# A four-layer gated transformer on one core: the conditional expert blocks of layer 0 moved ahead of the sure ones, three blocks added by one-hot matrices, and parts moved off GpSimd

## Chip, core and metric

The kernel runs on one core of a Trainium2 chip (trn2). The metric is the device time of one launch in microseconds (us). The engines are TensorE (PE; its weight loads are PEld), VectorE (DVE), ScalarE (ACT), GpSimd (POOL) and SyncE (SP, which here only issues transfers).

## The reference

The input x has 1024 rows of 256 numbers; four layers each add a gated attention to 64 context rows and a gated feed-forward (FFN) network. All is float32.

```python
for n in range(4):
    x = x + tanh(g_xattn[n]) * xattn[n](layernorm(x), ctx)
    x = x + tanh(g_ffn[n]) * ffn[n](layernorm(x))
```

- Layers 0 and 1: attention over a latent of 64 numbers, 16 heads. Layers 2 and 3: ordinary attention, 16 heads of 16, causal.
- FFN 0: a mixture of 16 experts of width 176. A softmax over the scores, a bias, the best 6 experts of each row, and two shared halves for all rows: `y = sum_e c[:, e] * ((silu(x W1 + B1) * (x W3 + B3)) W2 + B2)`.
- FFN 1: `gelu(x w1_q + b1) w2_q + b2`, the weights made ternary: `sign(w)` where `|w| >= 0.7 * mean|w|`, else 0; hidden width 1024.
- FFN 2: 8-bit weights and 8-bit rows: `round(x / s) @ round(w / t) * s * t + bias`, with `s = max|x| / 127` for each row.
- FFN 3: 8 experts of width 512, the best 2 of each row, and a shared expert.

## The kernel before

The stream x stays in SBUF as 8 tiles of 128 rows (`stream`, `x[t]`), two groups of four. The kernel is written in a tile framework that works out semaphores and buffer slots. It also orders the instructions of each engine at compile time, by priority in the order of the program, so an instruction may stand ahead of its place in the text where its inputs and slot are free. What is fixed is that each engine, and each queue of transfers, then runs in that order and waits at its first unready instruction. `behind(later, sooner)` orders two instructions by hand. The inside of a `tc.If` is ordered as one piece; all engines load the value and either run the piece or jump over it.

**The experts of layer 0.** Each row goes to 6 of 16 experts. The (row, expert) pairs are sorted on the chip into blocks of 128 rows of one expert: at least 55 blocks are never less than needed for this shape of data (`SURE0 = 55`), and up to 63 could be. `Experts.run(sure)` unrolls the sure blocks and then, under `tc.If(used > sure)`, the eight others; with these inputs the branch is jumped over. For each block:

- `fetch`: an indirect DMA on POOL gathers 128 rows with their 16 weights (`xs`), four blocks ahead.
- `turn`: PE transposes the rows, DVE copies them (`st`), DVE picks the block's weight, and PE loads the expert's address into a register (`value_load`).
- `up`: the bias as a one-hot product, two matmuls, SiLU on ACT, the product on DVE.
- `turn_hidden` and `down`: transpose, copy, the output product; the output `y` is copied into a ring of two times four tiles, and an indirect DMA on POOL adds it to rows in DRAM (`sums`). Layer 0 has two such sums, for even and odd blocks. The sum of the even ones starts as x plus the shared expert (`keep_rows`); blocks that add to the same sum wait for each other's landing.

Beside the blocks run steps of `fold1` (products of layer 1's attention weights, which PE makes) and of `ternary1` (layer 1's FFN weights made ternary on DVE: eight reductions of 128x512, one tiny matmul, then eight compares and eight selects). `between(i)` takes the next step after block i. After the branch both sums are read back into SBUF, on the queues of SP and ACT, added on DVE, and layer 1 begins.

Weights arrive through three slots of 1 MB (`C`): `used(name)` frees one and issues the next load on SP. PSUM tiles are `ps_mm` (one bank, four of them) and `ps_wide` (two banks, two of them).

**Attention.** `in_flight(scores, attend, gate, beside)` runs over the 8 tiles with three in flight: scores on PE, maximum and difference on DVE, exponential on ACT, sum and reciprocal on DVE, the product with it on POOL (L438), transposes on PE, copies on ACT, output products on PE. `beside` is work taken one step a tile.

**FFN 1.** The hidden layer is held as three bfloat16 terms whose sum is the float32 value (`three_terms`, L1491): the first term is a cast on ACT (L1493), the rest a subtraction on POOL (L1494), the second term a cast on DVE (L1495), the third a subtraction on DVE (L1496). The input of group 1 (`inputs(1)`) is prepared in the third quarter of group 0's up phase (L1557).

**FFN 2.** For each group: normalise on ACT, add the bias to the stream on POOL (L1634), the largest value of each row and its reciprocal on DVE (L1638 to L1640), scale and round on DVE (L1643, L1644), transposes, products (L1649), and the product with the row's scale is added to the stream (L457).

Of the kernel before, what the change touches and what calls it, by code (L numbers as in the profile page):

```python
# [37 lines left out]
P = 128  # L39
# [29 lines left out]
SURE0, SURE3 = 55, 20  # L69
W0U = 4 * F0  # L70
# [12 lines left out]
def tile_flamingo(ctx: ExitStack, tc: tile.TileContext, a: dict, out: bass.AP):  # L83
# [39 lines left out]
    def small(shape, name, bufs=3):  # L123
        return sb.tile(shape, F32, tag=name, name=name, bufs=bufs)
# [709 lines left out]
    def attention1(gate):  # L834
        weff, wvo = kept.pop("fold1")
        qcT = latents()
# [14 lines left out]
        latent_attend(qcT, wvo, gate, beside=queries(1))  # L851
# [133 lines left out]

    def keyed(layer, gate):
        beside = iter(())
        if layer == 2:
            values = region("wqk", 2048, "values")
            for _ in keys_values(2, region("weff", 2048, "kbd2"), values[:, :1024]):  # L990
                pass
            beside = keys_values(3, region("wvo", 2048, "kbd3"), values[:, 1024:])
# [175 lines left out]
    class Experts:  # L1168


        def __init__(self, route, xd, n, nb, stride, width, chunk, sums, w, bias, hTs, between):
# [4 lines left out]
            self.between = between  # L1176
            self.ring = [sb.tile([P, 4, D], F32, tag="xT", name="ring", bufs=2) for _ in range(2)]
# [5 lines left out]
        def fetch(self, b):  # L1183

            xs = sb.tile([P, D + self.experts], F32, tag="xn", name="xs", bufs=6)
# [8 lines left out]
        def turn(self, b):  # L1194
            st = t4([P, 1024], "blk")
            ps = ps_mm()
            for c in range(2):
                nc.tensor.transpose(ps[:, c * P : (c + 1) * P], self.xs[b][:, c * P : (c + 1) * P], ident)  # L1198
            nc.vector.tensor_copy(st[:, :D], ps[:, :D])  # L1199
# [15 lines left out]
                self.offset[0:1, b : b + 1], min_val=0, max_val=self.stride * (self.w.shape[1] // self.stride - 1)  # L1215
            )

        def up(self, b):
# [28 lines left out]
            nc.vector.scalar_tensor_tensor(s, lin, self.weight.pop(b), s, ALU.mult, ALU.mult)  # L1247
# [10 lines left out]
        def down(self, b):  # L1258
# [11 lines left out]
            if b % 2:  # L1270
                nc.vector.tensor_copy(y, ps[:, :D])
            else:
                nc.scalar.copy(y, ps[:, :D])  # L1273
            nc.gpsimd.indirect_dma_start(  # L1274
# [7 lines left out]
        def run(self, sure):  # L1282

            self.blocks(0, sure, self.between)
            used = nc.values_load(self.used, min_val=0, max_val=self.nb)
            with tc.If(used > sure):
                self.blocks(sure, self.nb, lambda i: None)

        def blocks(self, first, last, between):
            for b in range(first, min(first + 4, last)):  # L1290
                self.fetch(b)
            for i in range(first, last + 2):
                if i + 4 < last:
                    self.fetch(i + 4)
# [26 lines left out]
    def ffn0(gate):  # L1321
# [63 lines left out]
        used("L0_s13")  # L1385
        used("L0_s2")
# [11 lines left out]
        ternary = ternary1()  # L1398

        def between(i):  # L1400
            if i % 3 == 2 and not ended:
# [4 lines left out]
            if i > 32 and ended:  # L1406
                next(ternary, None)

        moe = Experts(placing, xd, E0, NB0, W0, F0, FC0, sums0, big[:, : E0 * W0], (bias_0, choice), hTs, between)
        moe.run(SURE0)  # L1410
        kept["fold1"] = ended[0]
        for t in range(NT):
            if t % TPG == 0:
                tiles = slice(t, t + TPG)
                nc.sync.dma_start(out=stream[:, tiles, :], in_=tiled(sums0[0], 0)[:, tiles, :])
                more = t4([P, TPG, D], "more")
                nc.scalar.dma_start(out=more, in_=tiled(sums0[1], 0)[:, tiles, :])
            if t % 2 == 0:
                two, its = slice(t, t + 2), slice(t % TPG, t % TPG + 2)
                done = nc.vector.tensor_tensor(stream[:, two, :], stream[:, two, :], more[:, its, :], ALU.add)  # L1420
        load_experts3(0, EARLY3, done)
        for _ in ternary:
            pass

    def ffn3(gate):
# [57 lines left out]
        moe = Experts(route[0], xd, E3, NB3, W3, F3, P, sums3, big, None, hTs, lambda i: None)  # L1483
        moe.run(SURE3)

# [5 lines left out]
    def three_terms(terms, v, rest):  # L1491

        nc.scalar.copy(terms[0], v)  # L1493
        nc.gpsimd.tensor_tensor(rest, v, terms[0], ALU.subtract)  # L1494
# [317 lines left out]
```

## Time and profile before

| | |
|---|---|
| device time, median of 3 runs | 948.43 us (945.85 to 948.74) |
| the profiled execution | 947.2 us, its span 945.4 us |
| mean granted clock of PE | 0.959 |
| busy: PE, PEld, DVE, ACT, POOL | 844.9, 547.3, 514.0, 288.7, 344.5 us |
| DMA | 75.15 MB, 38762 packets |

The stages, in us from the start of the span, as the rows of the timeline give them: attention 0 to about 212, routing and shared expert to 268, the sure blocks of layer 0 to 448, the sums read back to 475, attention 1 to about 570, FFN 1 to 625, attention 2 to 690, FFN 2 to 709, attention 3 to 760, FFN 3 to the end.

How to read the profile. "Busy" is the time in which an instruction of the engine ran; a matmul's end is modelled, so a busy PE is not a PE at its peak. A row of the timeline has start and duration in us, the engine, the line of the kernel, the operation, the tiles it writes and reads, the shapes, the number of instructions merged into the row, and in brackets the idle time of the engine before it and what ended it. A float32 matmul is two instructions in these rows, so that `x16` is eight products; a transpose is one. SPq, ACTq and POOLq are the queues in which transfers are issued.

### The profile page before, as it was taken

To read this page: it belongs to the slowest core of one execution; us is meant where nothing else is said; L and a number is where in the kernel's file an instruction comes from. 1 tells how busy PE (TensorE), PEld (TensorE's weight loads), DVE (VectorE), ACT (ScalarE), POOL (GpSimd) and SP (SyncE) were. 2 spreads that over 40 slices of the span, in tenths; PEclk is the share of its full clock that TensorE was granted. 3 is DMA by queue.
4 is the path that set the end of the run, shared out by engine and by line. 5 is a ranking of instruction groups with operands and counts; after the bars stand their busy time and mean duration, and the time that the engine had idled before them with its cause. 6 is when DMAs were issued, how large, how long until landed. Compare 5 with 4: busy or idle time off the path is not lost. (4 is left out here: it accounts for less than half of the span.)

```text
span 945.4 us, 12712 instructions
## 1 busy us (share of the span) xinstructions
PE 844.9 (89%) x4464; PEld 547.3 (58%) x4467; DVE 514.0 (54%) x1299; ACT 288.7 (31%) x561; POOL 344.5 (36%) x262
## 2 busy tenths in 40 slices
PE   5999999999999998899089997899869899999994
PEld 4544335876667875676045873665545556666662
DVE  4666457756934344573146765778777865222220
ACT  2221004433222332233013436516545531122221
POOL 0455452310066777787201232502312402144321
PEclk9999999999999998999589999989989999999997
DMA  9200228101156555654570000180000011122223
GB/s 359 93 16 22 79 65 258 52 18 32 56 158 161 125 121 128 156 86 71 117 266 1 1 1 1 42 302 2 1 23 1 1 47 58 40 47 48 38 23 66
DMA packets 38762, 75.15 MB, mean 79 GB/s; under 512 B 6240, under 2 KB 26706, under 8 KB 37322
## 3 DMA queue, kind: packets, MB, share of 16 engines
q1 hardware_dynamic: 23562, 52.01, 16.4%
q0 software_dynamic: 14496, 20.47, 12.9%
q10 hardware_dynamic: 640, 1.84, 0.5%
q8 instruction: 39, 0.64, 0.3%
q14 instruction: 25, 0.20, 0.1%
HBM read 58.73 MB, written 16.61 MB: 80 GB/s over the span
## 5 line engine op out<-in xcount | busy, mean ns | idle before, releaser
L438 POOL TENSOR_TENSOR attn<-attn,sm 128x1024 f32<-128x1024 f32 x32 | 60.8, 1901 | 197.1 <-DVE sm L437 163.9
L1247 DVE SCALAR_TENSOR_TENSOR blk<-wide,weight,blk 128x176 f32<-128x176 f32 (+1 forms) x75 | 37.0, 494 | 138.0 <-ACT blk L1246 137.9
L1274 POOL DMA_INDIRECT sums<-ring,big x55 | 87.5, 1590 | 34.9 <-issue 10.8
L422 PE MATMUL wide<-xT,big 128*128 128x512 f32 x192 | 88.3, 610 | 0.3 <-ACT big L557 0.3
L684 DVE TENSOR_TENSOR rope<-wide,big 128x512 f32<-128x512 f32 x96 | 59.6, 684 | 48.8 <-PE wide L422 47.5
L1227 PE MATMUL wide<-big,blk 128*128 x220 | 77.0, 472 | 0.1
L1186 POOL DMA_INDIRECT xs<-xd,big x55 | 55.1, 1001 | 55.8 <-DMA sums<-x 35.6
L1238 PE MATMUL wide<-big,blk 128*128 x160 | 72.2, 593 | 0.5 <-DVE blk L1199 0.5
L1246 ACT ACTIVATE blk<-wide 128x176 f32<-128x176 f32 (+1 forms) x75 | 29.4, 392 | 122.5 <-PE wide L1238 60.2
L422 PEld LDWEIGHTS wide<-xT,big 128*128 128x128 f32 x192 | 35.8, 193 | 47.6 <-issue 41.3
L657 PE MATMUL mm<-vo,attnT 128*128 128x256 f32 x256 | 58.6, 382 | 0.9 <-ACT attnT L453 0.9
L1262 PE MATMUL mm<-big,blk 88*128 x220 | 57.6, 384 | 0.5 <-ACT blk L1255 0.5
L407 PE MATMUL mm<-ident,xn 128*128 128x128 f32 x112 | 19.9, 322 | 41.5 <-DVE xn L395 35.4
L657 PEld LDWEIGHTS mm<-vo,attnT 128*128 128x128 f32 x256 | 47.4, 190 | 8.7 <-ACT attnT L453 2.9
L453 ACT COPY attnT<-mm 128x512 f32<-128x512 f32 x64 | 34.6, 589 | 54.7 <-PE mm L452 54.2
L1262 PEld LDWEIGHTS mm<-big,blk 88*128 88x128 f32 x220 | 42.0, 192 | 16.0 <-ACT blk L1255 1.4
L1227 PEld LDWEIGHTS wide<-big,blk 128*128 128x128 f32 x220 | 40.7, 196 | 13.3 <-issue 1.2
L436 DVE TENSOR_REDUCE sm<-attn 128x16 f32<-128x1024 f32 x32 | 38.8, 1213 | 16.3 <-ACT attn L430 13.7
L1186 POOL DMA_INDIRECT xs<-xd,scratch x20 | 19.5, 973 | 76.2 <-PE mm L1198 54.0
L1274 POOL DMA_INDIRECT sums<-ring,scratch x20 | 31.5, 1573 | 39.2 <-ACT ring L1273 16.8
L1238 PEld LDWEIGHTS wide<-big,blk 128*128 128x128 f32 x160 | 28.8, 190 | 28.9 <-issue 28.2
L407 PEld LDWEIGHTS mm<-ident,xn 128*128 128x128 f32 x112 | 15.1, 162 | 47.2 <-ACT rstd L383 27.6
(321 smaller groups left out, 1704.3 us busy)
## 6 DMA issues: line engine op xcount, KB each, us to landing
big<-in_L_w_gate_up SPq DMA_DIRECT2D x8, 1024.0 KB, 8.2
big<-in_L_w SPq DMA_DIRECT2D x4, 1408.0 KB, 7.9
big<-in_L_w_down SPq DMA_DIRECT2D x8, 512.0 KB, 9.3
w_L_qk<-in_L_qk SPq DMA_DIRECT2D x4, 896.0 KB, 8.7
big<-in_L_w SPq DMA_DIRECT2D x4, 704.0 KB
big<-in_L_wo SPq DMA_DIRECT2D x1, 2048.0 KB, 12.9
xd<-xn SPq DMA_DIRECT2D x16, 128.0 KB, 1.8
sums<-x SPq DMA_DIRECT2D x16, 128.0 KB, 1.8
```

The lines of the kernel that those rows point to most:

```text
L407: nc.tensor.transpose(ps[:, i * P : (i + 1) * P], n[:, c * P : (c + 1) * P], ident)
L422: nc.tensor.matmul(ps, w(c), xT[:, c, :], start=(c == 0), stop=(c == 1))
L436: nc.vector.tensor_reduce(sm, e, AX.X, ALU.add)
L438: nc.gpsimd.tensor_tensor(e, e, sm.unsqueeze(2).to_broadcast([P, groups, n]), ALU.mult)
L657: nc.tensor.matmul(ps[:, :D], aT[:, s, :], vo[:, s, :], start=(s == 0), stop=(s == NP - 1))
L684: nc.vector.tensor_tensor(m[:, s, :].rearrange("q (b t) -> q b t", t=S), ps[:, s, :].rearrange("q (b t) -> q b t", t=S), table, ALU.mult,)
L1186: nc.gpsimd.indirect_dma_start(out=xs, out_offset=None, in_=self.xd, in_offset=bass.IndirectOffsetOnAxis(ap=self.gather[:, b : b + 1].bitc ...
L1227: nc.tensor.matmul(ps[:, 0, : 2 * n], st[:, c * P : (c + 1) * P], self.w[:, bass.ds(r + c * 2 * n, 2 * n)], start=False, stop=(c == 1),)
L1238: nc.tensor.matmul(ps[:, k, :n], st[:, c * P : (c + 1) * P], self.w[:, bass.ds(r + (2 * c + k) * n, n)], start=(c == 0), stop=(c == 1),)
L1247: nc.vector.scalar_tensor_tensor(s, lin, self.weight.pop(b), s, ALU.mult, ALU.mult)
L1262: nc.tensor.matmul(ps[:, :D], hT[:, j * P : (j + 1) * P], self.w[: self.chunk, bass.ds(r + j * D, D)], start=(j == 0), stop=(j == self.n - 1),
L1274: nc.gpsimd.indirect_dma_start(out=self.sums[b % len(self.sums)], out_offset=bass.IndirectOffsetOnAxis(ap=self.scatter[:, b : b + 1].bitca ...
```

## The change

- `run` fetches the first four blocks, loads `used`, puts the `tc.If` with the eight rare blocks there, and runs the sure blocks after it (layer 0 alone, `hot > 0`; layer 3 keeps its order). Rare blocks are fetched one at a time into a slot of their own.
- In both expert layers the offsets of eight blocks at a time are copied into a small tile (`near`) behind the copy of the block's rows, and the register is loaded from it.
- The outputs of the last three sure blocks of layer 0 (`HOT0`) are not scattered. `hit` makes a one-hot matrix of 128 x 8 x 128 for each, beside blocks 27, 32 and 37; `collect` reads both sums back, all on SP, and adds them; `add` multiplies the one-hot matrices with the three outputs, two tiles of the stream to a PSUM bank, and adds the product to the stream.
- `ternary1` moves from the sure blocks to attention 1. `fold1` takes a step every fourth block from block 5, not every third. `used` of the shared expert's two weights comes after block 3.
- `three_terms` subtracts on DVE and casts every second second term on ACT; `inputs(1)` comes one quarter sooner.
- FFN 2: the rounding of group 0 is taken into the steps beside attention 2; the row's scale is multiplied in before the transposes, the bias is a one-row matmul in front of the products, and nothing is on POOL.

```diff
+HOT0 = 3
     def attention1(gate):
+        ternary = ternary1()
-        latent_attend(qcT, wvo, gate, beside=queries(1))
+        latent_attend(qcT, wvo, gate, beside=zip_longest(queries(1), ternary))
+        for _ in ternary:
+            pass
...
+    def beside2(keys):
+        for i in range(NT + 3):
+            if i == NT + 1:
+                kept["rounded"] = rounded(0)
+            next(keys, None)
+            yield
...
     class Experts:
         def turn(self, b):
-            nc.vector.tensor_copy(st[:, :D], ps[:, :D])
+            copied = nc.vector.tensor_copy(st[:, :D], ps[:, :D])
+            if b < self.sure and b % 8 == 0:
+                n = min(8, self.sure - b)
+                self.near = small([1, 8], "near", 2, I32)
+                behind(nc.vector.tensor_copy(self.near[:, :n], self.offset[0:1, b : b + n]), copied)
+            offset = self.near[:, b % 8 : b % 8 + 1] if b < self.sure else self.offset[0:1, b : b + 1]
...
         def down(self, b):
+            if b in self.hits:
+                self.held.append((self.hits.pop(b), y))
+                return
...
+        def hit(self, b, room, after=None):
+            base, step = self.rows
+            row, at = small([P, 1], "row"), small([P, NT], "at")
+            copied = nc.vector.tensor_copy(row, self.scatter[:, b : b + 1])
+            nc.vector.tensor_scalar(at, base, row, -1.0 / step, ALU.subtract, ALU.mult)
+            for h, first in room:
+                n = h.shape[1]
+                nc.vector.tensor_tensor(
+                    h,
+                    place.unsqueeze(1).to_broadcast([P, n, P]),
+                    at[:, first : first + n].unsqueeze(2).to_broadcast([P, n, P]),
+                    ALU.is_equal,
+                )
+            return room
...
+        def add(self, held):
+            for t in range(0, NT, 2):
+                ps = ps_mm()
+                for u in (t, t + 1):
+                    for i, (hits, y) in enumerate(held):
+                        h = next(h[:, u - v, :] for h, v in hits if v <= u < v + h.shape[1])
+                        at = (u - t) * D
+                        nc.tensor.matmul(ps[:, at : at + D], h, y, start=(i == 0), stop=(i == len(held) - 1))
+                two = stream[:, t : t + 2, :]
+                nc.vector.tensor_tensor(two, ps.rearrange("p (u d) -> p u d", u=2), two, ALU.add)
...
-        def run(self, sure):
-            self.blocks(0, sure, self.between)
+        def run(self, sure, collect=None):
+            self.sure = sure
+            for b in range(4):
+                self.fetch(b)
+            if not self.hot:
+                self.blocks(0, sure, self.between, 4)
             used = nc.values_load(self.used, min_val=0, max_val=self.nb)
             with tc.If(used > sure):
-                self.blocks(sure, self.nb, lambda i: None)
+                self.blocks(sure, self.nb, lambda i: None, 0)
+            if self.hot:
+                self.blocks(0, sure, self.between, 4)
+                collect()
+                self.add(self.held)
...
     def ffn0(gate):
-        used("L0_s13")
-        used("L0_s2")
         def between(i):
-            if i % 3 == 2 and not ended:
+            if i == 3:
+                used("L0_s13")
+                used("L0_s2")
+            if i > 4 and i % 4 == 1 and not ended:
 ...
-            if i > 32 and ended:
-                next(ternary, None)
+        def collect():
+            more = [t4([P, TPG, D], "more") for _ in range(NG)]
+            for g in range(NG):
+                nc.sync.dma_start(out=stream[:, groups[g], :], in_=tiled(sums0[0], 0)[:, groups[g], :])
+            for g in range(NG):
+                nc.sync.dma_start(out=more[g], in_=tiled(sums0[1], 0)[:, groups[g], :])
+            for t in range(0, NT, 2):
+                two, its = slice(t, t + 2), slice(t % TPG, t % TPG + 2)
                added.append(
                    nc.vector.tensor_tensor(stream[:, two, :], stream[:, two, :], more[t // TPG][:, its, :], ALU.add)
                )
...
     def three_terms(terms, v, rest, scalar):
         nc.scalar.copy(terms[0], v)
-        nc.gpsimd.tensor_tensor(rest, v, terms[0], ALU.subtract)
-        nc.vector.tensor_copy(terms[1], rest)
+        nc.vector.tensor_tensor(rest, v, terms[0], ALU.subtract)
+        (nc.scalar.copy if scalar else nc.vector.tensor_copy)(terms[1], rest)
         nc.vector.tensor_tensor(terms[2], rest, terms[1], ALU.subtract)
...
-                if g == 0 and f2 == 2:
+                if g == 0 and f2 == 1:
                     xT.append(inputs(1))
-                three_terms([hidden[:, g, k, 2 * f2 : 2 * f2 + 2, :] for k in range(3)], h, h)
+                three_terms([hidden[:, g, k, 2 * f2 : 2 * f2 + 2, :] for k in range(3)], h, h, f2 % 2 == 1)
...
+    def rounded(g):
...
+            nc.vector.tensor_scalar(n, n, xi[:, i : i + 1], ROUND, ALU.mult, ALU.add)
+            nc.vector.tensor_scalar(n, n, ROUND, xs[:, i : i + 1], ALU.subtract, ALU.mult)
...
     def ffn2(gate):
-            nc.gpsimd.tensor_tensor(tiles, tiles, bias_2.unsqueeze(1).to_broadcast([P, TPG, D]), ALU.add)
-                nc.vector.tensor_scalar(n, n, xi[:, i : i + 1], 127.0, ALU.mult, ALU.min)
-                nc.vector.tensor_scalar(n, n, ROUND, ROUND, ALU.add, ALU.subtract)
+            xqT = transposed(kept.pop("rounded") if g == 0 else rounded(g))
+                nc.tensor.matmul(ps[:, :D], ones[:1], bias_2, start=True, stop=False)
-                gated_add(g * TPG + i, ps[:, :D], xs[:, i : i + 1])
+                nc.vector.tensor_tensor(x[t], ps[:, :D], x[t], ALU.add)
```

## The prediction

> **What bounds the kernel now.** I read the 40 slices of the page first: TensorE (PE) is busy in tenths of 9 almost throughout, except in the slice from 449 us, where its digit is 0, in two 8s from 354 us, and in a 7, two 8s and a 6 between 567 and 709 us. So what the change is worth has to come from these places or from the layer-0 expert loop in front of slice 19. Next I read busy time by stretch, the columns being PE, PEld, DVE, ACT, POOL, clock, DMA share, GB/s:
>
> ```profile
> 268.00:300.00 32.00, 31.18 (x208) 23.11 (x209) 11.89 (x46) 8.26 (x23) 18.26 (x17) 0.95 0.69 188
> 340.00:400.00 60.00, 53.47 (x256) 37.62 (x256) 26.22 (x89) 16.16 (x45) 43.84 (x35) 0.94 0.61 135
> 448.40:475.50 27.10, 0.00 (x0) 0.02 (x1) 6.44 (x23) 2.19 (x4) 6.24 (x5) 0.54 0.52 125
> 570.20:602.70 32.50, 24.33 (x101) 10.54 (x104) 18.44 (x22) 21.29 (x32) 11.50 (x6) 0.95 0.00 1
> ```
>
> The 55 sure blocks run from 268 to 448.3 us. PE is full until 340 (40.00 of 40 from 300 on); after that it loses 6.5 us in 60. POOL carries two indirect DMAs a block (gather about 1.0 us, scatter 1.59, each after 0.30 of issue: 3.2 us a block), PE 2.65 us a block plus the fold of layer 1. The two are close, and POOL falls behind. From 448.3 to 475.5 PE does nothing. The timeline says why:
>
> ```profile
> 448.33 0.37 ACT L1273 COPY ring<-mm 128x256 f32<-128x256 f32 x1 [1.22 <-PE mm L1262]
> 448.94 1.55 POOL L1274 DMA_INDIRECT sums<-ring,big  x1 [0.50 <-issue]
> ...
> 456.54 1.55 POOL L1274 DMA_INDIRECT sums<-ring,big  x1 [1.17 <-DMA sums<-ring,big]
> 462.12 0.81 SPq L1415 DMA_DIRECT2D x<-sums  x2
> ...
> 468.47 1.29 DVE L1420 TENSOR_TENSOR x<-x,more 128x512 f32<-128x512 f32 x2 [21.75 <-DMA more<-sums]
> ...
> 475.51 2.10 PE L407 MATMUL mm<-ident,xn 128*128 128x128 f32 x8 [27.21 <-DVE xn L395]
> ```
>
> The last output leaves PSUM at 448.7, but four scatters are still queued on POOL; the last one starts at 456.54, the sums are read back at 462.12, landed at 468.47, normalised, and PE starts again. That chain ends last here.
>
> **Part by part,** against the profiled execution (span 945.4, device time 947.2; the median shown is 948.43, 1.2 more).
>
> **Three blocks not scattered, no branch behind them.** Blocks 52 to 54 stay in SBUF, so POOL's last scatter is block 51, which today starts at 448.94 (four remain after the copy: 51, 52, 53, 54). Chain: 448.94 + 3.9 (median landing of L1274) = 452.8; read-back 6.35 (462.12 to 468.47) gives 459.2; then the 7.04 us from there to PE, and two to four more adds of 128x512 (L1420, 0.69 each) = 467.6 to 469.0 against 475.5. That is 6.5 to 7.9 us won. The four loads now stand all on SP, where the two of the even sums go as soon as block 50 has landed; I count 0. The one-hot product is 8 tiles x 3 blocks x 2 passes of 0.216 us (L657: 16 in 3.46 us) = 10.4 us of PE, from 448.7 to 459.1: hidden by the wait for the read-back that ends at 459.2. If that cover is gone, the 10.4 us are themselves the tail, and it lasts to about 461 instead of 475.5 (15 less). The three hits are 1.2 us each on DVE (a 128x1024 operation, L429), which idles half of the loop. Taken -7, bounds -3 (landing as slow as the 5.6 us from 456.54 to 462.12, adds all in front) and -15.
>
> **The branch ahead.** All engines load `used` (ready at 231.4, L1144) and jump over eight unrolled blocks between the fourth gather and block 0. Nothing in the trace shows a jump alone. In layer 3 SP and ACT issue 2.26 us after POOL's last scatter has ended (936.76 to 939.02), in layer 0 4.03 us after (458.09 to 462.12), with a landing in both: the jump costs 0 to 4. On the other side, if engines join there with everything the skipped blocks need (the stored rows L372 of 267.49 land 6.1 us later, at 273.6) and jump then, block 0 starts at 277.6 instead of 268.8: +9. PE waits for it, and behind POOL's jump queue the gathers 4 and up. Taken +3, by the row of layer 0 (4.0) less the idle of 1.0 us that PE has at 267.94 today.
>
> The Trainium skill (Runtime: NRT & Kernel Launch, Instruction fetch mechanics) says that a taken branch to a target outside the two pages held forces a fetch before execution goes on; that speaks against moving a jump from a place covered by a DMA wait to one that is not. It gives no time for the stall, so by it the term is above 0 and no more.
>
> **Layer-1 ternary weights out of the loop.** 8 reductions (0.68), 8 compares (0.52), 8 selects (0.75), small ones 0.8: 16.4 us of DVE leave the loop. What they cost there is POOL, in two ways:
>
> ```profile
> 389.90 1.61 POOL L1274 DMA_INDIRECT sums<-ring,big  x1 [3.10 <-DVE sums L1513]
> ...
> 415.50 1.79 POOL L1274 DMA_INDIRECT sums<-ring,big  x1 [0.30 <-DVE blk L1247]
> ```
>
> The reduction waits 3.3 us for its weights and holds everything behind it in DVE's queue, so a scatter starts 2.8 late; and five gathers and scatters between 414 and 425 take 0.1 to 0.2 more than their fellows at 0.99 and 1.59 (0.8 in sum). Loop -4; bounds 0 (PE is the pace then) and -8 (with the 3.6 us that the clock of 0.94 costs in 340 to 400). Fold steps every fourth block instead of third move PE work, not its amount. In attention 1 the 16.4 us meet 14.0 us of idle DVE up to 500 and 17.1 up to 557, while PE is full: +1, bounds 0 and +5 (a third of it in front of a softmax).
>
> **Late registers.** One copy of 8 integers on DVE per 8 blocks, at 0.2 us; PE then loads a register after that copy, not long before. Taken 0 (seven of eight values are there early); see the rivals.
>
> **Loads moved on SP.** `used` of the two shared-expert weights now comes after block 3, so two loads of the fold's inputs (issued at 255.25 and 265.76, 7.6 us to landing) go out between 270, when their slots are free, and 280, and land by 288; the first fold step comes with block 5, near 287. Taken 0; a late landing holds PE by up to 3, within the bounds of the branch. With the fold ending at block 49, the loads for layers 1 and 2 go out up to 40 us later and stand in SP's queue ahead of the read-back, behind the slot that the last fold step frees, about 14 us before the last block. Taken 0: the read-back waits for block 50's scatter anyway.
>
> **FFN 1 without GpSimd.** Two groups by line of DVE, and then two rows of PE's timeline:
>
> ```profile
> L1496 DVE TENSOR_TENSOR big<-h,big 128x1024 bf16<-128x1024 f32 x8 | 13.4, 1672 | 0.2
> L1495 DVE CAST big<-h 128x1024 bf16<-128x1024 f32 x8 | 11.2, 1404 | 12.2 <-POOL h L1494 12.2
> ```
>
> ```profile
> 586.27 1.02 PE L1565 MATMUL mm<-xT,w_L_w 128*128 128x512 bf16 x4 [3.45 <-DVE more L1548]
> ...
> 596.27 0.81 PE L1565 MATMUL mm<-more,w_L_w 128*128 128x512 bf16 x3 [1.68 <-DVE more L1550]
> ```
>
> The same cast takes 0.69 alone and 2.6 beside L1494 on POOL; the subtraction 1.22 and 3.03. That is 9.3 us of DVE in which it stands still: (11.2 - 8 x 0.69) + (13.4 - 8 x 1.22). Now DVE takes the eight subtractions itself (+9.8) and gives four casts to ACT (-2.8 on DVE, +4.2 on ACT). DVE's total falls by only 2.3, but L1548 and L1550 no longer stand behind a stalled cast: the two PE waits go, 5.1 us, and with them part of the 3 us in which matmuls run 0.43 instead of 0.215 apart after 586. Against it stands ACT, 2.35 to 3.4 us per pair of feature blocks beside PE's 2.58. Taken -5, bounds -1 (ACT is next) and -9.
>
> **FFN 2.** Group 0 is rounded within attention 2, the bias becomes a one-row matmul, and POOL's 2.34 us adds (L1634) go.
>
> ```profile
> 691.03 1.48 DVE L1639 TENSOR_SCALAR xs<-xs 128x4 f32<-128x4 f32 x1
> ...
> 693.72 1.96 PE L407 MATMUL mm<-ident,xn 128*128 128x128 f32 x8 [4.44 <-DVE xn L1644]
> ```
>
> L1639 takes 1.48 here, beside L1634 on POOL, and 0.16 in group 1: 1.3 us on the path. The wait of 4.44 in front of group 0's transposes is what its earlier rounding can take away; group 1's chain then no longer queues behind it on DVE (1.7 us, L384 at 694.62 after the root at 692.93). Added: 8 x 2 x 0.216 = 3.5 us of bias matmuls, half under the wait for group 1, and 4.2 us of DVE within attention 2, where DVE is busy 46 of 62 us. Taken -4, bounds 0 and -7.
>
> Sum: -7 + 3 - 4 + 1 + 0 - 5 - 4 = -16; 947.2 - 16 = 931.2, and with the profiled run 1.2 under the median, 932. The bounds, taken as independent, give 920 to 942.
>
> **Rivals.** *The front eats the tail:* the branch costs its +9 and the loop stays POOL's; -7 + 9 + 0 + 1 - 5 - 4 = -6, 942. For it: PE has no other work at 268; against: the register is known 36 us before. *PE sets the pace:* POOL keeps up, block 51 has landed before the last block is done, and only the 10.4 us of one-hot matmuls remain: -15 + 3 - 6 + 1 - 5 - 4 = -26, 922. Against it: 7 scatters remain after the last gather at 434.03, at 2.1 us each. *Slower, by the late registers:* if each `value_load` now stands on PE between the transposes and the matmul that uses it and waits for DVE, every block of both expert layers pays a hand-over. The smallest hand-overs to PE in the loop are 0.20 to 0.53 us (L1253 after L1247); at 0.33 x 75 blocks this is 25 us: 932 + 25 = 957. It decides from 16 / 75 = 0.21 us a block. Against it: eight offsets come with one copy, and PE's loop shows no gap for register loads today.
>
> **Numbers.** Forecast 0.46, front 0.20, PE's pace 0.12, late registers 0.22. Measured differences under 0.3% (2.8 us) count as none. Faster: 0.45 of the forecast, 0.15 of the front case, all of PE's pace, 0.72. Same: 0.01, 0.03, and 0.03 of the late registers, 0.07. Slower: the rest, 0.02 of the front case and 0.19 of the late registers. The range must take in the forecast and the front case, the upper half of PE's pace and the lower part of the late registers: 919 to 954.
>
> **What would show it.** Right: the last L1274 of layer 0 within 1 us of PE's last block, one-hot matmuls behind it, PE's gap of 27.2 down to about 20, less the 10.4 that they fill; the cast L1495 at 0.69 each; no POOL row in FFN 2. Wrong: PE idle for over 4 us between the shared expert and block 0, more than 2.8 us a block where there is no fold, PE waits for DVE in attention 1 that are not there now, or ACT as releaser of L1565.

## The result, and the profile after

The changed kernel takes 942.69 us in the median of 20 runs (935.47 to 949.27), the kernel before 948.59 (945.25 to 959.39): ratio 0.9937, 95% interval 0.9921 to 0.9954, some 6 us faster. The forecast was 932, 16 faster: the sign and the range held, the size did not. Three later comparisons, each on a chip of its own, gave 0.9963 (0.9935 to 0.9991), 0.9941 (0.9913 to 0.9968) and 0.9929 (0.9900 to 0.9959).

First the stages that the prediction was built on, as busy time by stretch of the changed kernel; columns as before (PE, PEld, DVE, ACT, POOL, clock, DMA share, GB/s).

```profile
267.20:300.00 32.80, 29.41 (x147) 20.82 (x149) 11.71 (x49) 7.67 (x22) 19.65 (x17) 0.86 0.55 120
340.00:400.00 60.00, 57.21 (x299) 42.70 (x298) 28.27 (x100) 17.41 (x49) 45.79 (x35) 1.00 0.61 132
452.70:465.90 13.20, 10.35 (x49) 8.79 (x47) 7.14 (x19) 1.95 (x3) 0.00 (x0) 1.00 0.67 229
566.20:592.40 26.20, 23.67 (x102) 11.09 (x104) 20.90 (x28) 23.23 (x33) 0.00 (x0) 0.93 0.00 1
```

The gap behind the last block is 13.2 us instead of 27.1, and 10.35 of it is work; the up phase of FFN 1 is 26.2 us instead of 32.5 with no POOL in it. So two stages gained more than the whole change did. Where did it go? One profile each is too little for that, so the next table has the stages of two profiles of the kernel before and of four of the changed kernel, cut at TensorE's rows (first transposes of a layer, first product of a phase).

| stage, us | before | changed | mean difference | forecast |
|---|---|---|---|---|
| start to layer 1's first transpose | 475.5, 476.5 | 465.9, 468.1, 467.7, 465.8 | -9.1 | -8 |
| attention 1 | 94.7, 95.0 | 100.3, 100.5, 100.1, 100.5 | +5.5 | +1 |
| FFN 1 | 54.5, 54.6 | 47.3, 46.2, 46.2, 46.2 | -8.0 | -5 |
| attention 2 | 64.6, 64.6 | 64.7, 64.0, 65.9, 64.0 | 0 | 0 |
| FFN 2 | 20.8, 20.9 | 22.4, 26.6, 22.4, 26.6 | +3.7 | -4 |
| attention 3 | 51.4, 51.4 | 51.4, 51.5, 54.5, 51.5 | +0.8 | 0 |
| FFN 3 to the end | 184.0, 184.0 | 185.2, 186.7, 186.3, 188.1 | +2.6 | 0 |
| span | 945.4, 946.8 | 937.2, 943.8, 943.0, 942.7 | -4.4 | -16 |

Attention 1 and FFN 2 hold 12 of the missing 12 us; layer 3 adds 3, FFN 1 and layer 0 gave 4 more than forecast. Now the lines behind each. The end of layer 0, in the timeline of the changed kernel:

```profile
448.79 1.54 POOL L1300 DMA_INDIRECT sums<-ring,big  x1 [0.79 <-PE mm L1276]
...
450.42 1.10 SPq L1479 DMA_DIRECT2D x<-sums  x2
...
452.50 10.53 PE L1334 MATMUL mm<-ring,hits 128*128 128x256 f32 x48
...
453.03 0.81 SPq L1481 DMA_DIRECT2D more<-sums  x2
...
458.69 2.50 DVE L1485 TENSOR_TENSOR x<-x,more 128x512 f32<-128x512 f32 x4 [7.60 <-DMA more<-sums]
...
465.88 1.64 PE L409 MATMUL mm<-ident,xn 128*128 128x128 f32 x8 [2.85 <-DVE xn L397]
```

The last scatter leaves at 448.79, while the last block still runs; its landing and the read-back end at 458.69 and are covered by the one-hot products. This is the chain that the prediction wrote down, within 2 us of it at every step (its 448.94, 452.8, 459.2 and 467.6 stand beside the rows at 448.79, 453.03, 458.69 and 465.88).

Attention 1, its last 20 us, same view:

```profile
547.16 0.28 PE L1596 MATMUL mm<-sums,ones 128*128 128x2 f32 x2
...
549.50 3.18 DVE L1600 TENSOR_SCALAR nthr<-thr 128x2 f32<-128x2 f32 x1
...
552.72 0.49 DVE L1605 TENSOR_SCALAR low<-w_L_w,nthr 128x512 f32<-128x512 f32 x1
...
563.40 0.48 DVE L1605 TENSOR_SCALAR low<-w_L_w,nthr 128x512 f32<-128x512 f32 x1
563.54 1.12 PE L1701 MATMUL mm<-ident,wq 128*128 128x128 f32 x4 [5.20 <-DVE wq L1695]
```

The eight reductions were done by 478.5, but the tiny product that makes the threshold of them stands in TensorE's order at 547.16, in step with the tiles. So all eight comparisons and selections come behind it, from 552.72 to 564.86, mixed with the weights of layer 2, and TensorE waits 5.20 us for VectorE, a wait that is not there before.

FFN 2, TensorE's rows:

```profile
682.08 0.69 PE L1732 MATMUL mm<-kept,ones 1*128 1x256 f32 x2
682.70 1.13 PE L1734 MATMUL mm<-kept,xT 128*128 128x256 f32 x4
...
688.29 0.44 PE L409 MATMUL mm<-ident,xn 128*128 128x128 f32 x2 [2.77 <-DVE xn L1721]
688.65 0.69 PE L1732 MATMUL mm<-kept,ones 1*128 1x256 f32 x2
689.28 0.69 PE L409 MATMUL mm<-ident,xn 128*128 128x128 f32 x2
689.90 1.22 PE L1732 MATMUL mm<-kept,ones 1*128 1x256 f32 x2
```

The first half no longer waits (4.44 us before), the second does: 2.77 us. One of the one-row products of the bias falls into the rest of that wait (688.65); the others cost 0.52 to 0.63 us each (682.08 to 682.70), and one 1.15 at the half clock that follows.

### The profile page after: what moved, and what is told of

It reads as the page before. It is cut to its first block, busy times and chain, and to the rows that moved or that the text cites. A ratio compares the mean times of both kernels' runs of the same rounds, so it can differ in the third digit from the quotient of the medians.

```text
span 937.2 us, 12881 instructions
## 1 busy us (share of the span) xinstructions
PE 858.9 (92%) x4528; PEld 558.2 (60%) x4531; DVE 521.8 (56%) x1328; ACT 292.3 (31%) x565; POOL 315.7 (34%) x247
## 4 chain that ended last, share of the span: by engine, by line
PE 72%; DVE 12%; DMA 5%; ACT 4%; issue 3%; POOL 2%; SPq 0%; POOLq 0%; ACTq 0%; DVEq 0%
PE wide L424 9%; PE wide L1261 7%; PE mm L1285 7%; PE wide L1250 6%; PE mm L424 4%; PE mm L659 4%; PE wide L1529 2%; PE mm L1662 2%; PE wide L644 2%; PE mm L1646 2%; DMA sums<-ring,big 2%; PE mm L454 2%; PE mm L1276 2%; PE wide L940 2%; PE mm L1216 2%
## 5 line engine op out<-in xcount | busy, mean ns | idle before, releaser
L1300 POOL DMA_INDIRECT sums<-ring,big x52 | 83.2, 1599 | 28.8 <-issue 10.0
L1250 PE MATMUL wide<-big,blk 128*128 x220 | 79.4, 479 | 11.0 <-DVE near L1221 6.5
L1261 PE MATMUL wide<-big,blk 128*128 x160 | 72.6, 594 | 2.5 <-DMA sums<-x 2.1
L1204 POOL DMA_INDIRECT xs<-xd,big x55 | 54.6, 992 | 60.3 <-DMA sums<-x 35.7
L1250 PEld LDWEIGHTS wide<-big,blk 128*128 128x128 f32 x220 | 40.9, 198 | 26.2 <-issue 15.4
L1217 DVE COPY blk<-mm 128x256 f32<-128x256 f32 x75 | 31.4, 420 | 16.7 <-PE mm L1216 13.3
L454 PE MATMUL mm<-ident,attn 128*128 128x128 f32 x256 | 34.7, 280 | 6.2 <-POOL attn L440 6.1
```

What stands on the lines that cost most here:

```text
L454: nc.tensor.transpose(ps[:, i * P : (i + 1) * P], ev[:, pr * P : (pr + 1) * P], ident)
L1204: nc.gpsimd.indirect_dma_start(out=xs, out_offset=None, in_=self.xd, in_offset=bass.IndirectOffsetOnAxis(ap=self.gather[:, b : b + 1].bitc ...
L1250: nc.tensor.matmul(ps[:, 0, : 2 * n], st[:, c * P : (c + 1) * P], self.w[:, bass.ds(r + c * 2 * n, 2 * n)], start=False, stop=(c == 1),)
L1261: nc.tensor.matmul(ps[:, k, :n], st[:, c * P : (c + 1) * P], self.w[:, bass.ds(r + (2 * c + k) * n, n)], start=(c == 0), stop=(c == 1),)
L1300: nc.gpsimd.indirect_dma_start(out=self.sums[b % len(self.sums)], out_offset=bass.IndirectOffsetOnAxis(ap=self.scatter[:, b : b + 1].bitca ...
```

## The experiments

Each kernel differs from the changed one by its edit alone, unless it says otherwise. The ratio is to the kernel before, on the same chip.

**The changed kernel again** (three chips), and the kernel before for a second profile. The "wait at block 48" is a wait of TensorE, in front of an up product, for the register that comes out of the copied offsets (`near`); its rows follow under "Registers straight from the list".

> The changed kernel again, beside its variants. Ratio to before 0.992 to 0.995. Theory (the order of each engine is fixed, so its waits come back): TensorE waits 4 to 6 us for the small copy of offsets at block 48, and attention 1 lasts 99 to 101 us. Rival (the wait at block 48 was one execution's chance, a landing that was late once): that wait is under 2 us here, and the loop is 3 us or more shorter than its 185.4.

> The changed kernel beside the next kernels. All theories: ratio 0.993 to 0.997, layer 1 starts at 465 to 471 us, attention 1 lasts 99 to 101, the up phase of FFN 1 25 to 27.

> The changed kernel beside it. All theories: ratio 0.993 to 0.997; attention 1 99 to 101 us, layer 1 starts at 465 to 471.

> The kernel before, for a second profile of its stages. All theories: attention 1 94 to 96 us, FFN 1 up 32 to 33, FFN 2 20.5 to 21.5, layer 1 starts 19 us after the last scatter, at 473 to 479.

Medians 945.81, 942.97 and 944.08 us; the ratios and the stages are above. The wait at block 48 came back each time (5.6 to 6.0 us): it is in the order of the engines, not chance. What differs from run to run is FFN 2 (22.4 or 26.6) and attention 3 (51.4 or 54.5); the last section says by what.

**The threshold first.**

```diff
+        any(next(ternary) for _ in range(9))
         latent_attend(qcT, wvo, gate, beside=zip_longest(queries(1), ternary))
```

> The reductions, the tiny product and the first comparison of the ternary weights are taken ahead of attention 1's tiles. Theory (the tiny product stood at the end of TensorE's order, so all comparisons came when the stage was ending): the product moves from 547 us to about 482, no wait of TensorE for the weights of layer 2 (it was 5.2), attention 1 lasts 94 to 97 us instead of 100.3, the whole is 4 to 6 us under the changed kernel, ratio 0.988 to 0.990. Rival (VectorE lacks the room for 16.4 us anywhere in this stage, so what is moved holds a softmax instead): attention 1 stays at 99 to 101, the difference is within 1.5 us.

940.87 us, ratio 0.9918 (0.9888 to 0.9948), 4.9 under the changed kernel on its chip. Timeline:

```profile
487.49 0.28 PE L1596 MATMUL mm<-sums,ones 128*128 128x2 f32 x2
...
488.48 0.17 DVE L1600 TENSOR_SCALAR nthr<-thr 128x2 f32<-128x2 f32 x1
488.69 0.49 DVE L1605 TENSOR_SCALAR low<-w_L_w,nthr 128x512 f32<-128x512 f32 x1
```

With the product 60 us sooner the comparisons fall into VectorE's pauses, no wait for L1695 is left, and attention 1 lasts 95.7 us. The theory held for the stage, though the ratio is above its 0.988 to 0.990: the room was there, as the forecast had counted; the order did not use it.

**Registers straight from the list.**

```diff
-                behind(nc.vector.tensor_copy(self.near[:, :n], self.offset[0:1, b : b + n]), copied)
-            offset = self.near[:, b % 8 : b % 8 + 1] if b < self.sure else self.offset[0:1, b : b + 1]
+            offset = self.offset[0:1, b : b + 1]
```

> The registers are loaded straight from the list of offsets, as before; nothing else differs from the changed kernel. Theory (the late registers cost only where VectorE is held, at block 48, and there what TensorE could still have done, half an up product and one down product): 2 to 3 us under the changed kernel. Rival 1 (a hand-over in every block, 0.1 us or more of 75): 7 us or more under it. Rival 2 (the register loads go in a bunch ahead of block 0 and hold TensorE there; seven late ones of eight cost nothing): 0 to 3 us over it.

943.19 us, ratio 0.9927 (0.9894 to 0.9959), 2.6 under the changed kernel, within the intervals. TensorE's waits from 264 to 456 us (total, times, longest), first here, then in the changed kernel:

```profile
PE mm L1216 <- PEq L1346: 8.0, 1, 8.0
PE mm L1285 <- DVE ring L1294: 4.7, 3, 2.2
```

```profile
PE wide L1250 <- DVE near L1221: 6.5, 2, 5.6
...
PE wide L1250 <- DMA sums<-x: 1.9, 1, 1.9
PE mm L1216 <- DVEq L1346: 1.6, 1, 1.6
```

Both halves of the theory and rival 2 are seen at once. Without the copies TensorE waits 8.0 us at the branch (L1346) for its own sequencer, where it waits 1.6 with them, and layer 1 starts at 471.0 instead of 465.8 to 468.1. That register loads which depend on no copy are ordered ahead of the branch is the likely reason; the profile does not list register loads, so it is not shown one by one. With the copies the loop pays 6.5 us of waits. In layer 3 the first up product waits 2.1 us with the copies and 0.5 without.

**The fold every third block.** `i % 4 == 1` becomes `i % 3 == 2`.

> The fold of layer 1 takes a step every third block from block 5, so it ends at block 38 and not 49. Theory (the loads of the layer 1 and layer 2 weights at 415 to 418 us met the scatters and made one land 5 us after its issue, which held the gather of block 49, VectorE and the copy of offsets behind it): the loads go out near 385, the wait at block 48 falls from 5.6 to under 2 us, the loop lasts 179 to 182 us instead of 185.4, ratio 0.988 to 0.991. Rival (GpSimd is late there whatever the loads do, since the fold's steps are denser and leave it behind sooner): the wait moves to another block and the loop stays over 184.

945.31 us, ratio 0.9964 (0.9939 to 0.9988), no difference. The wait for the copy at block 48 fell to 2.1 us, but the loads now went out from 388.5 to 390.6, and a wait of 4.4 us for VectorE ended at 398.5; the last scatter left at 452.9. The wait goes with the loads, as the theory has it: a scatter issued at 391.3 took 7.4 us to land, one issued at 421.6 in the second profile of the changed kernel 7.6, where most take 3.8 to 4.3. The last scatter leaves no sooner by the move, as the rival has it.

**The branch behind the blocks.**

```diff
-            if not self.hot:
-                self.blocks(0, sure, self.between, 4)
+            self.blocks(0, sure, self.between, 4)
             with tc.If(used > sure):
...
             if self.hot:
-                self.blocks(0, sure, self.between, 4)
                 collect()
```

> Only the branch of the eight rare blocks is put behind block 54 again; three outputs are still held and added by one-hot matrices. Theory (in three profiles of the branch ahead the first scatter leaves at 279.8 to 282.4 us, with 277.0 before; GpSimd's chain of gathers and scatters then takes 167 to 172 us whatever else is changed, and layer 1 starts 17 us after its last scatter): the first scatter leaves at 277 to 279, layer 1 starts 17 to 19 us after the last one, as the jump is covered by that scatter's landing; 2 to 4 us under the changed kernel. Rival (the forecast's: a jump behind the last block stands on the path, 4 us, and the front gives back 3): 0 to 2 us over it, layer 1 starts 20 us or more after the last scatter.

945.23 us, ratio 0.9961 (0.9930 to 0.9992): within the changed kernel's ratios. Timeline:

```profile
444.16 1.54 POOL L1299 DMA_INDIRECT sums<-ring,big  x1 [0.77 <-ACT blk L1277]
...
450.94 0.81 SPq L1478 DMA_DIRECT2D more<-sums  x2
...
465.87 2.10 PE L409 MATMUL mm<-ident,xn 128*128 128x128 f32 x8 [5.20 <-DVE xn L397]
```

The first scatter leaves at 275.5 instead of 281.3 and the last at 444.2, but layer 1 starts 21.7 us behind the last one instead of 16.4, since the odd sums are read 6.8 us after that scatter's issue and not 4.2. Theory and rival each had one end right: the branch costs about 6 us in front or 5 behind, and its place is worth 1 us (465.9 against 466.9, the mean of four profiles).

**The bias by VectorE.** One addition of 128x1024 for each half, behind its rounding:

```diff
-                nc.tensor.matmul(ps[:, :D], ones[:1], bias_2, start=True, stop=False)
+            added = nc.vector.tensor_tensor(four, four, bias_2.unsqueeze(1).to_broadcast([P, TPG, D]), ALU.add)
+            behind(added, kept["turned", g])
```

> FFN 2's bias is added to the stream by VectorE, one 128x1024 addition for each half behind its rounding, and not by one-row products; the rest is the changed kernel. Theory (a one-row product of 256 columns holds TensorE for 0.62 us like a full one, eight of them 5.0 us, and the ones between the transposes of the second half run at half the pace): FFN 2 lasts 18 to 20 us instead of 22.4 to 26.6, 3 to 5 us under the changed kernel. Rival (the second half's rounding on VectorE sets the end of FFN 2, and two more additions of 1.2 us lengthen it): FFN 2 22 us or more, no difference or up to 2 us over.

940.32 us, ratio 0.9914 (0.9887 to 0.9942). FFN 2 lasts 20.3 us, TensorE's rows:

```profile
682.77 3.72 PE L1735 MATMUL mm<-kept,xT 128*128 128x256 f32 x16 [0.56 <-ACT xT L135]
691.56 2.21 PE L409 MATMUL mm<-ident,xn 128*128 128x128 f32 x8 [5.06 <-DVE xn L1721]
694.17 6.25 PE L1735 MATMUL mm<-kept,xT 128*128 128x256 f32 x16 [0.39 <-ACT xT L135]
```

The one-row products are gone, and what is left is the length of the stage before the change (20.8): the wait of 4.44 in front of the first half is now one of 5.06 in front of the second.

**FFN 2 as before,** its edit being the removed lines of the diff put back.

> FFN 2 and what was taken into attention 2 for it are as before the change; the rest is the changed kernel. Theory (the change made FFN 2 1.6 to 5.8 us longer, not 4 shorter): FFN 2 lasts 20 to 21.5 us, attention 2 64 to 65, the whole is 1 to 4 us under the changed kernel. Rival (the forecast's: the earlier rounding saves 4 us, and the longer stage seen is the clock's chance): 2 to 5 us over it.

939.64 us, ratio 0.9917 (0.9895 to 0.9940). FFN 2 21.2 us, attention 2 64.5: the theory. By these two stages the part that was forecast at -4 makes the kernel 1.4 to 4.9 us slower; the intervals of the whole (this one and the changed kernel's 0.9921 to 0.9954) overlap.

**One output held.** `HOT0 = 1`.

> One output is held and added by a one-hot matrix, not three (blocks 52 and 53 are scattered). Theory (the end of the layer is 17 us behind GpSimd's last scatter, and two more scatters at 2.5 us each come before it): 4 to 6 us over the changed kernel, TensorE idle 6 us or more between the last block and layer 1. Rival (TensorE paces this end, with 3.5 us of one-hot products per held block): 5 to 7 us under it.

950.03 us, ratio 1.0010 (0.9986 to 1.0034). Layer 1 starts at 476.0, TensorE idle 15.8 us in front of it, 18.0 behind the last scatter: the theory. The held blocks are worth what their scatters cost POOL.

**The subtractions on GpSimd again.**

```diff
-        nc.vector.tensor_tensor(rest, v, terms[0], ALU.subtract)
+        nc.gpsimd.tensor_tensor(rest, v, terms[0], ALU.subtract)
```

> FFN 1's eight subtractions of the three terms are on GpSimd again; the split casts and the earlier input of the second half stay as in the change. Theory (VectorE stands still beside GpSimd's pass): VectorE's cast goes from 0.69 to 1.4 us in the mean, its last subtraction from 1.22 to 1.6, the up phase of FFN 1 lasts 29 to 33 us instead of 25.2 to 26.9, 3 to 7 us over the changed kernel. Rival (the earlier input and the casts on ScalarE brought the gain): the up phase stays under 27.5, within 1.5 us.

948.72 us, ratio 1.0003 (0.9976 to 1.0030), but the up phase lasts 26.3 us as in the change, while VectorE stands still more than ever (groups by line, mean ns of one behind the comma):

```profile
L1576 DVE TENSOR_TENSOR big<-h,big 128x1024 bf16<-128x1024 f32 x8 | 16.6, 2092 | 0.1
...
L1575 DVE CAST big<-h 128x1024 bf16<-128x1024 f32 x4 | 6.6, 1649 | 2.6 <-POOL h L1574 2.6
```

In the changed kernel these are 1216 and 692. So the stall is as the theory has it, and it is not what TensorE waits for in this kernel: the rival, in the up phase. Of the 3 to 6 us by which the whole is over the changed kernel, the down phase (22.0) shows 0.9 and attention 2 (66.6) 2.0; the rest lies in layer 0, which the edit does not touch, and stays open.

**The second half's input late** (in the changed kernel) **and early** (in the kernel before), `f2 == 1` or `f2 == 2`:

> The changed kernel, but the second half's input of FFN 1 is prepared in the third quarter of the up phase again. Theory (the earlier input is what takes TensorE's waits away): the up phase lasts 28 to 32 us, waits for the second half's input of 3 us or more are back, 2 to 5 us over the changed kernel. Rival (the subtractions on VectorE and the casts on ScalarE do it): the up phase stays at 25 to 27.

> The kernel before, with one edit: the second half's input of FFN 1 is prepared one quarter sooner; the subtractions stay on GpSimd. Theory (this edit alone brings the gain): the up phase lasts 26 to 28.5 us instead of 32.5, 4 to 6 us under the kernel before, ratio 0.993 to 0.996. Rival (the forecast's: VectorE's stalled casts cause the waits): the up phase 31 us or more, ratio 0.998 to 1.001.

Late: 944.12 us, ratio 0.9953 (0.9929 to 0.9977), up phase 26.3 us. Early in the kernel before: 947.54, ratio 0.9986 (0.9959 to 1.0014), up phase 30.9 instead of 32.5. So the early input alone brings 1.6 us; with the subtractions on VectorE its place does not matter; with them on GpSimd it still comes to 26.3 when half of the casts are on ScalarE as well. Either way is enough, and the gains of the two do not add. But every kernel with an up phase under 27 us also has half of the casts on ScalarE, and the two with 30.9 and 32.5 have them all on VectorE. No run moved the casts alone, so it stays open whether they do most of it.

**Both mends together,** then with FFN 2 as before, then with the branch behind and the registers straight from the list:

> The changed kernel with the threshold of the ternary weights first and with FFN 2's bias added by VectorE. Theory (the two lie in different stages and add up): attention 1 95 to 97 us, FFN 2 20 to 21, ratio to before 0.985 to 0.989. Rival (the later layers take back what is won, as TensorE's clock falls with fewer pauses): ratio 0.990 or more, with the mean clock lower than in the changed kernel.

> The changed kernel with the threshold first and with FFN 2 as before the change. Theory (the earlier rounding of the first half only moves the wait to the second half's rounding, so FFN 2 as before and FFN 2 with the bias on VectorE are worth the same): FFN 2 20 to 21.5 us, ratio within 0.002 of the kernel with the bias on VectorE. Rival (the earlier rounding is worth the 4 us of the forecast, once the one-row products are gone): 3 us or more over that kernel.

> The same as the one before, and the branch behind the blocks with registers loaded straight from the list: of the change to layer 0 only the three held outputs, the slower fold and the moved ternary weights remain. Theory (the branch ahead holds the first scatter 5 us and gives back 2.5 to 4.7 behind the last one; without it the copied offsets have no use): the first scatter leaves at 275 to 278 us, layer 1 starts at 463 to 466 instead of 466 to 470.5, 1 to 4 us under the kernel before in this list, ratio 0.982 to 0.986. Rival (early register loads cost TensorE without a branch too): TensorE waits more than 3 us for its sequencer in the blocks, no gain.

938.35 us (0.9924, 0.9900 to 0.9948), 940.48 (0.9916, 0.9887 to 0.9945) and 940.42 (0.9925, 0.9902 to 0.9947): the same to what can be measured. The stages are as expected (attention 1 95.5, 96.8, 96.9; FFN 2 20.1, 20.6, 20.7), the sum is not below 0.990, though the mean clock is hardly lower (0.964 to 0.966, with 0.964 to 0.972 in the changed kernel). Attention 3 took back 1.5 us in the first; the second and third had layer 1 start at 470.5 and 470.4, late for their kind. The third's first scatter left at 279.5 and not at 275 to 278, so the branch's place showed no worth here either. Its branch again holds TensorE for its sequencer, 4.4 us in front of the one-hot products (L1344), where the kernel with the branch behind and the copies waits 0.9; that is the rival's wait, though not in the blocks but behind them.

**The offsets two blocks ahead,** with both mends:

```diff
-            if b < self.sure and b % 8 == 0:
+            first = 0 if b == 0 else b + 2
+            if first < self.sure and first % 8 == 0:
```

> Threshold first, FFN 2's bias on VectorE, and the offsets of eight blocks copied two blocks before the first of them needs one (the first eight still at block 0). Theory (the wait at block 48 stands on TensorE, but GpSimd's last scatter sets the end of layer 0): no wait of TensorE for the copy of offsets over 1 us; layer 1 still starts 16 to 17.5 us behind the last scatter, at 466 to 471; 5 to 9 us under the changed kernel, no more than the two mends. Rival (that wait holds gathers and scatters too, so that POOL's chain is shorter by it): layer 1 starts at 461 to 465, 9 to 13 us under the changed kernel.

934.42 us in six runs, ratio 0.9829 (0.9782 to 0.9876), the lowest of all, 9.7 under the changed kernel on the same chip. In its profile no wait for the copy is left, and TensorE ends its last block 4.7 us sooner; layer 1 starts all the same 16.6 us behind the last scatter, at 465.4 against 465.8. The theory held for the place, and its 5 to 9 us were a little short: the profiles differ by 9.3, to which attention 1 brings 4.7 and FFN 2 6.4 (20.2 against 26.6), while FFN 1 and attention 3 give some 3 back. About 4 of FFN 2's 6.4 are the clock's: two of the changed kernel's four profiles have 22.4 there.

## Why the prediction was right and wrong

**Layer 0: the terms held, by POOL's clock.** Means of the first, 52nd and last scatter are 277.7, 449.4 and 457.0 before, 281.3 and 450.5 in the change. The branch was put at +3: the first scatter leaves 3.5 later. That it fits is partly luck: with the branch alone moved back the first scatter left 5.7 sooner and layer 1 followed the last one 5.3 later, so the place is worth more at either end than was forecast and nearly nothing in sum. The loop was put at -4 for the ternary weights: first to 52nd scatter 169.2 us instead of 171.6, -2.4. The tail was put at -7: the last scatter leaves 7.6 sooner relative to the 52nd, and layer 1 follows it after 16.4 instead of 19.0, -10.2. Sum -9.1, forecast -8. Cut at TensorE's last block instead, the same profiles read as a loop 6 us longer (185.2 instead of 179.0) and a tail 15 us shorter (12.8 instead of 27.5), and these largely cancel, for TensorE's last block is not what layer 1 waits for: in fourteen profiles with the branch ahead and three blocks held, with the wait for the copied offsets and without it, layer 1 starts 15.9 to 17.9 us behind the last scatter.

**Late registers: 0 was right for layer 0 by luck.** The rival's hand-over in every block is not there. But one block in eight has its register behind its own rows' copy, and where VectorE stood still for 4.97 us in front of L1227 and so of that copy, TensorE waited 5.6 for an integer. It cost next to nothing, for POOL was later still (with the wait away layer 1 started at 465.4 instead of 465.8 on the same chip). In layer 3 it cost 1.6 (2.1 against 0.5). The forecast had only asked what the copy costs, not what the register's new place stands behind.

**Attention 1, +1: the step that failed first.** The idle time of VectorE was counted rightly (14.0 us up to 500), and with the threshold first it sufficed. What was missed is that the steps depend on one another through another engine: eight reductions, one product on TensorE, then everything else; and one step a tile puts that product at the ninth. The wait measured 5.2 us; the bound had been +5.

**FFN 2, -4: the step that failed most.** "The wait of 4.44 is what its earlier rounding can take away" was right for the first half, and the second half's rounding, whose input is ready no sooner than attention 2's last tile (added at 678.59 in the changed kernel's profile), ends last in its place: 5.06 us where nothing fills it. The bias was put at 3.5 us, half of it hidden: eight products at 0.43, twice the 0.216 of L657. Here they took 0.52 to 0.63 each and 1.15 once, 5.3 in all, and only one fell into the wait. The Trainium skill (TensorE: Matmul & The Clock Gate, Why this matters for your kernels) says that a single product over 32 rows takes the same time as one over 128. At full clock one over a single row took 0.52 to 0.63 us in this stage and one over 128 rows 0.48 to 0.53, which agrees; so the forecast was right to take a full product's price, and the price itself was too low for this stage.

**FFN 1, -5: inside its bounds (-8.0, bound -9), the reason not shown.** The stall beside GpSimd is real, and the waits go when it goes. They also go with the stall still there, when the input is made sooner and half of the casts leave VectorE; and in every run in which they went, half of the casts had left it.

**After FFN 2, put at 0: +3.4.** 0.8 is attention 3, where one of the four profiles lost 3 us to a spell of half clock. In FFN 3 1.6 is the register. About 1.5 more lies behind TensorE's last product: from there to the end it is 12.3 and 12.4 us before and 13.2 to 14.5 in the change. GpSimd's last scatter waits longer for the landing of the one before it (the row before the change, then in it):

```profile
935.21 1.55 POOL L1274 DMA_INDIRECT sums<-ring,scratch  x1 [2.90 <-DMA sums<-ring,scratch]
```

```profile
927.33 1.54 POOL L1300 DMA_INDIRECT sums<-ring,scratch  x1 [4.36 <-DMA sums<-ring,scratch]
```

The wait is 2.90 to 3.02 us in the three profiles without the change to the experts and 4.01 to 4.66 in all seventeen with it, so it comes with the change; by what stays open. The clock takes 0.8 off: two of the four profiles lack a spell of half clock that FFN 3 had before.

## What to carry to other kernels

Find the engine whose chain sets the end and measure along it: a stage cut at another engine's last instruction shows gains and losses that cancel. When work is moved beside other work, count the room, and then follow the moved chain's dependences through every engine on which the order is fixed. When a wait is taken away in front of one half, ask when the other half's input is ready, for the wait is often just handed on.

## What the chip showed that was not expected

After a pause of under 3 us TensorE ran at half clock for 7 to 17 us. FFN 2 of the changed kernel's second profile, busy time by stretch (the clock is the third column from the end):

```profile
686.00:690.00 4.00, 1.24 (x5) 0.68 (x4) 3.70 (x16) 0.30 (x1) 0.00 (x0) 0.84 0.00 0
690.00:694.00 4.00, 3.75 (x11) 1.72 (x10) 0.82 (x4) 1.36 (x3) 0.00 (x0) 0.50 0.00 0
694.00:698.00 4.00, 4.00 (x9) 2.81 (x10) 1.51 (x4) 1.31 (x3) 0.00 (x0) 0.50 0.02 4
698.00:702.00 4.00, 4.00 (x9) 1.87 (x8) 1.81 (x7) 0.00 (x0) 0.00 (x0) 0.50 0.00 0
702.00:706.00 4.00, 4.00 (x13) 3.25 (x14) 1.32 (x4) 0.78 (x2) 0.00 (x0) 0.52 0.00 0
```

The pause was 2.76 us, and the clock stayed at half for 17 us (688.7 to 705.8 by these stretches), in 12 of which TensorE was busy throughout; in the first profile a pause of 2.77 was followed by about 7. That is the difference between 22.4 and 26.6 us in FFN 2: the same pause costs 4 us more in one execution than in another. The 54.5 of attention 3 is the same kind of luck: in that profile the clock is 0.50 from 718 to 722, behind a pause of 1.63 us that the other three have too, without half clock. What sets a spell off is not shown: in the second profile one begins after 620 (clock 0.56 from 620 to 624), and no pause in the 15 us before it was longer than 0.8 us. The Trainium skill (TensorE: Matmul & The Clock Gate, HAM oscillation — how this bites in real kernels) bars idle gaps above about 3.4 us, and in its section What's actually happening it gives the way back as about 3.4 us of sustained work in a free-running window. Here the half clock came after shorter pauses, and 12 us of unbroken work did not end it. The other surprise is the wait at the branch when the registers are loaded straight from the list: 8.0 us against 1.6 in front of the blocks, 4.4 against 0.9 behind them.
